# Scale rows loaded earlier, another matmul order in a wave's last step, and four normalizations moved to VectorE

## The chip, the cores and the metric

The kernel runs on one core of a Trainium2 chip. The metric is the device time of one execution in microseconds (us); the time before is 2232.88 us, the median of 3 runs (2232.68 to 2235.79). The profile is of one execution, with a span of 2227.6 us.

## What is computed

Input `u` has 2048 rows (tokens) of 1024. Three residual layers follow each other, each on the normalized rows:

```
x = u
x = x + 0.5 * ffn(layernorm(x))
x = x + s4(layernorm(x))
x = x + 0.5 * ffn(layernorm(x))          # the same weights as in the first

ffn(x) = (silu(x @ Wg) * (x @ Wu)) @ Wd  # Wg, Wu: 1024 x 2752, Wd: 2752 x 1024
W[k, n] = scale[k // 128, n] * (w4[k, n] - (z4[k // 128, n] + 1))
```

The weights of the feed-forward layers are packed 4-bit integers; each group of 128 rows of a weight has a scale and a zero point of its own for each column. `s4` is a causal convolution along the 1024 columns with a kernel that is computed from a state-space model's parameters, plus a multiple of its input.

## The kernel before

**Jobs.** The rows are cut into four blocks of 512. A job is one feed-forward layer of one block; `JOBS` (L1159) lists eight: first layers of blocks 0 and 1, then their last layers, then the same for blocks 2 and 3. `fast` (L1161) walks through them. Each has an up part (`gate_up`, L526) and a down part (`down`, L603). Smaller work is hung onto their steps as hooks: `at(up, s, f)` runs `f` as step `s` of the up part is written, `at(dn, s, f)` the same in the down part. The convolution of a block's middle layer, the residual adds and the normalization for the next job are such hooks.

**Group scales as ratios.** The products of a group of 128 rows must be scaled by that group's scale. The kernel multiplies the running sum in PSUM by the ratio of this group's scale to the next one's, after each group. So after each step each sum is read from its PSUM bank, multiplied and written back (`scaled`, L520), on ScalarE or on VectorE in turn. The ratios are in the table `rat`, made by `scales` (L288): TensorE transposes rows of scales that `scale_rows` (L281) loaded, VectorE copies them (L306), guards and inverts them (L277 to L279) and multiplies neighbours (L311, L312).

**Waves and steps.** The 2752 columns of gate and up are 21 blocks of 128 and a half one. A wave is three blocks of gate and the same three of up (waves 0 to 4), or two and two (waves 5 to 7; wave 7 has the half block as a fifth unit). Each such 128-column unit has one of six PSUM banks. A wave has eight steps, one for each group of 128 rows. In a step each unit gets two products: the input is split into a high part (fp32r, tile `xTh`) and a low rest (fp16, `xTl`), and each is multiplied with the weights. The order of these is the list `turns` (L543 to L545): for the first half of the units low, then high; for the second half high, then low. So a six-unit step is written as three low, six high and three low products. A unit is scaled when its second product is done.

**The end of a wave.** In a wave's last step (`g == GK - 1`) the units aren't scaled but go in pairs to `gated` (L576): ScalarE makes silu of the gate (L578), VectorE multiplies it with the up unit into `hf` (L581), GpSimd makes a rounded copy `hh` (L583) and the rest `hl` (L585). `hf` has two buffers, `g` three. The next wave's units take the banks in the same order.

**The down part** has 44 steps: for each half of the output columns one step for each of 22 blocks, with four sums of 128 columns, each of two products (`hl`, `hh`) and a scaling.

**Job 0** also makes the weights. Packed rows are loaded and split into nibbles on VectorE, reduced by the zero points (`dequantize`, L432; `dequantize_down`, L465) and written to DRAM (`wq`, `wdq`), from where every job's steps load them, four steps ahead. `first_weights` (L475) sets the steps at which this happens. The ratios are hooks of job 0 as well: for blocks 0 to 2 in `start` (L1270), for blocks 3 to 8, 9 to 14 and 15 to the end at steps 4, 20 and 36 (L1210), with the rows loaded in the same hook. They are first needed at steps 8 (wave 1), 24 (wave 3) and 40 (wave 5).

**Normalizing the next block.** `normalized` (L188) subtracts the mean and multiplies by the inverse deviation, a 128 x 1024 tile at a time, on an engine that can be given. For the next job's first layer `anorm` (L1233) calls it at the down steps; in job 0 (`pool`) it runs on GpSimd, and so does the split into high and low parts in `turn` (L204, `by_pool`); in the other jobs on VectorE. TensorE then transposes the tile (L198).

**Order.** The program is written in one order, and a framework places the instructions of each engine: it takes those that it reckons ready, the earlier written first, so that the placed order can differ from the written one. It also sets all waits. Where the order has to be kept, `in_order_of_writing` (L120) adds dependences along an engine; `start` runs under it for ScalarE, VectorE and SyncE.

Of the kernel before, what the change touches and what calls it, by code (L numbers as in the profile page):

```python
# [16 lines left out]
ALU = mybir.AluOpType  # L17
# [13 lines left out]
GK = 8  # L31
GD = 21
TW = 6
WIDE = INTER // P
# [18 lines left out]
def macaron_s4_kernel(  # L53
# [31 lines left out]
    nc = tc.nc  # L85
# [34 lines left out]
    def in_order_of_writing(f, *engines):  # L120

        start = len(nc.cur_bb.bb.instructions)
        f()
        written = list(nc.cur_bb.bb.instructions)
        for e in engines:
            last = next((i for i in reversed(written[:start]) if i.engine == e), None)
            for ins in written[start:]:
                if ins.engine == e:
                    if last is not None:
                        tc.add_manual_dep(  # L130
                            ins,
                            last.name,
                            mybir.DependencyInfo(
                                mybir.DependencyClass.NoSync, mybir.DependencyReason.DATA
                            ),
                            reason="order of writing",
                        )
                    last = ins


    x = {}
# [43 lines left out]
        for t in range(NT):  # L185
            ln[b, t] = (mv[:, t, 0:1], r[:, t : t + 1], k)

    def normalized(b, t, engine=nc.vector):  # L188
        m, r, k = ln[b, t]
        n = t4(f"xn_{b}_{k}_{t}")  # L190
        engine.tensor_scalar(n, x[b][t], m, r, ALU.subtract, ALU.mult)  # L191
        return n

    def turned(n, name, bank=bank):
# [331 lines left out]
    def gate_up(j, b, hooks):  # L526
        hi, lo = pieces[b]
        ps = {}
        ready = {s: load_w(j, s) for s in range(AHEAD)}
        for s, (wi, g) in enumerate(STEPS):  # L530
            if s + AHEAD < len(STEPS):
                ready[s + AHEAD] = load_w(j, s + AHEAD)
            for hook in hooks.get(s, ()):
                hook()
            w = ready.pop(s)
            fs = WAVES[wi]
            n = len(fs)
            order = [(2 * f + i, i * n + u) for u, f in enumerate(fs) for i in range(2)]
            if wi == len(WAVES) - 1:
                order.append((2 * WIDE, 2 * n))  # L540


            early = len(order) // 2  # L543
            turns = [(k, pos, k == 1) for k in range(2) for pos in range(early)]
            turns += [(k, pos, k == 0) for k in (1, 0) for pos in range(early, len(order))]  # L545
            for k, pos, done in turns:
                unit, col = order[pos]
                if g == 0 and unit not in ps:
                    ps[unit] = acc(f"pg_{j}_{unit}")
                p = ps[unit]  # L550
                weights = w[:, bass.ts(col, P)]
                if k == 0:

                    weights = weights.bitcast(BF16).rearrange("p (n k) -> p k n", k=2)[:, 1, :]
                nc.tensor.matmul(  # L555
                    p,
                    weights,
                    (lo, hi)[k][:, g, :],
                    start=(g == 0 and not done),
                    stop=(g == GK - 1 and done),  # L560
                    skip_group_check=True,
                )
                if not done:
                    continue
                if g < GK - 1:
                    on_act = unit % 2 == 0 or (j == 0 and pos == 1)
                    if unit == 2 * WIDE:
                        on_act = g % 2 == 0
                    scaled(on_act, p, p, rat[:, unit, g : g + 1])
                elif unit == 2 * WIDE:  # L570
                    gated_half(j, ps.pop(unit))
                elif unit % 2:
                    gated(j, unit // 2, ps.pop(unit - 1), ps.pop(unit))
        pieces.pop(b)
# [586 lines left out]
    def fast():  # L1161
        for j, (b, k) in enumerate(JOBS):
            prev = JOBS[j - 1] if j else None
            after = JOBS[j + 1] if j + 1 < len(JOBS) else None
            up, dn = {}, {}

            def at(hooks, s, f):
                hooks.setdefault(s, []).append(f)

            if prev:  # L1170
                pb, pk = prev
                for t in range(NT):
                    at(up, t, lambda t=t: back(pb, 1, t))
                if pk == 1:
                    late = 30 if j == 1 else 0
                    at(up, 4, lambda: moments(pb, 2))
                    at(up, 5, lambda: deviations(pb, 2))
                    s4x, s4n = {}, {}

                    def norm(t):  # L1180
                        s4n[t] = normalized(pb, t)

                    def swap(t):
                        s4x[t] = turn_whole(s4n.pop(t), f"st_{pb}_{t}")

                    def conv(t):
                        convolve(pb, t, s4x.pop(t), f"{pb}_{t}")

                    for t in range(NT):
                        at(up, late + 8 + 4 * t, lambda t=t: norm(t))  # L1190
                        at(up, late + 10 + 4 * t, lambda t=t: swap(t))
                        at(up, late + 12 + 4 * t, lambda t=t: conv(t))
                    at(up, late + 27, lambda: moments(pb, 3))
                    at(up, late + 28, lambda: deviations(pb, 3, LIFT))

                    def save():
                        for t, dst in enumerate(saved(pb)):
                            nc.sync.dma_start(dst, x[pb][t])

                    at(up, late + 28, save)  # L1200
                else:

                    def store():
                        for t, dst in enumerate(rows_of(out, pb)):
                            nc.sync.dma_start(dst, x[pb][t])
                        x.pop(pb)

                    at(up, 4, store)
            if j == 0:
                for s, k0, k1 in ((4, 3, 9), (20, 9, 15), (36, 15, WIDE)):  # L1210
                    at(up, s, lambda k0=k0, k1=k1: scales(k0, k1, scale_rows(k0, k1)))
                at(up, 40, scales_down)
                for t in range(NT):
                    at(up, t, lambda t=t: in_order_of_writing(lambda: second_half(t), *STARTING))
                first_weights(up, dn, at)
            if j == 1:
                tables = s4_tables()
                for s in range(2, 42):
                    at(up, s, lambda: next(tables, None))
            if j == 2:  # L1220
                at(up, 30, in_order)
            if after:
                ab, ak = after
                if ak == 1:
                    at(up, 55 if j == 0 else 6, lambda: load_x(ab, rows_of(u, ab)))
                    stage, o = (dn, 0) if j == 0 else (up, 44)
                    at(stage, o, lambda: in_order_of_writing(lambda: moments(ab, 1), ET.DVE))
                    at(stage, o + 1, lambda: deviations(ab, 1, LIFT))
                an = {}

                pool = j == 0

                def anorm(t):  # L1233
                    an[t] = normalized(ab, t, nc.gpsimd if pool else nc.vector)

                o = 3 if j == 0 else 0
                for t in range(NT):
                    at(dn, o + 1 + 4 * t, lambda t=t: anorm(t))
                    at(dn, o + 2 + 4 * t, lambda t=t: turn(ab, t, an[t][:, :512], 0, by_pool=pool))
                    at(dn, o + 4 + 4 * t, lambda t=t: turn(ab, t, an[t][:, 512:], 1, by_pool=pool))  # L1240
            at(dn, 21, lambda: load_x(b, rows_of(u, b) if k == 1 else saved(b)))
            for t in range(NT):
                at(dn, NF + 5 + 4 * t, lambda t=t: back(b, 0, t))
            gate_up(j, b, up)
            down(j, b, dn)
        b = JOBS[-1][0]
        for t, dst in enumerate(rows_of(out, b)):
            back(b, 1, t)
            nc.sync.dma_start(dst, x[b][t])

    STARTING = ET.Activation, ET.DVE, ET.SP
# [18 lines left out]
    def start():  # L1270
# [5 lines left out]
        srow = scale_rows(0, 3)  # L1276
        zeros_down = zero_words(1)
        fetch(1)
        zero_points(0, zeros)
        fetch_zeros(0)  # L1280
        fetch_zeros(1)
# [17 lines left out]
            less_mean(t, 1)  # L1299
        scales(0, 3, srow)  # L1300
        zero_points(1, zeros_down)

    in_order_of_writing(start, *STARTING)
    x.pop(0)
    fast()
    x.clear()
# [85 lines left out]
```

## Time and profile before

| | |
|---|---|
| time | 2232.88 us |
| TensorE busy | 2121.1 us of 2227.6 |
| VectorE busy | 1705.0 us |
| ScalarE busy | 1431.1 us |
| GpSimd busy | 383.4 us |
| scaling of gate and up sums, ScalarE (L522) | 1264 at 661 ns |
| the same on VectorE (L524) | 1144 at 695 ns |
| hf on VectorE (L581) | 168 at 749 ns |
| hh and hl on GpSimd (L583, L585) | 168 each, at 640 and 1345 ns |

In the profile's lines PE is TensorE, DVE VectorE, ACT ScalarE, POOL GpSimd; PEld is TensorE loading weights, SPq the queue of SyncE, which issues most DMAs. A line of the timeline has the start in us, the busy time in us, engine, line of the code, operation, what is written and what is read, the number of instructions merged into it, and in brackets the idle time before it and what ended that. A line of the waits has who waited and for whom, the sum in us, how often, and the longest. An answer on one tile has for each form the shortest, median and longest duration in ns. Matmuls are pipelined and overlap in the records, so that a step is measured from start to start.

### The profile page before, as it was taken

The numbers are of one execution on the slowest core, as the hardware profiler recorded it, in microseconds if no ns is written. First come the engines' busy times: TensorE is split into PE (matmuls) and PEld (weight loads), VectorE is DVE, ScalarE is ACT, GpSimd is POOL, SyncE is SP. The second block draws the span as 40 slices with busy tenths as digits, with TensorE's granted clock in tenths as the row PEclk, the third lists the DMA queues.
The fourth block names the chain that finished last, engine by engine and source line by source line (L and its number), as shares of the span: only waits on it lengthen the run. The fifth ranks groups of instructions, "written<-read, shape, count | busy, mean of one in ns | idle before, by whom it ended". The sixth has DMA issues, their size and how long they took to land.

```text
span 2227.6 us, 28004 instructions
## 1 busy us (share of the span) xinstructions
PE 2121.1 (95%) x9524; PEld 1424.2 (64%) x9524; DVE 1705.0 (77%) x2799; ACT 1431.1 (64%) x2245; POOL 383.4 (17%) x393
## 2 busy tenths in 40 slices
PE   5888889999999999999999999999999999999998
PEld 3444565566777657755685557776587765865576
DVE  7887768867886878777877788867788677777776
ACT  6667667545764577666766667646776467766675
POOL 0222511221001220022102220012300122012210
PEclk9999989999999999999999999999999999999999
DMA  7777675424443544543645454434444354454443
GB/s 251 255 248 264 200 237 167 154 93 145 145 154 115 174 137 151 190 141 115 211 152 180 128 167 133 154 117 158 137 133 156 117 172 137 156 190 142 131 133 121
DMA packets 163669, 359.93 MB, mean 162 GB/s; under 512 B 22395, under 2 KB 27572, under 8 KB 163518
## 3 DMA queue, kind: packets, MB, share of 16 engines
q1 hardware_dynamic: 162670, 356.50, 49.6%
q8 instruction: 78, 1.28, 0.2%
q10 hardware_dynamic: 592, 1.16, 0.1%
q0 software_dynamic: 256, 0.39, 0.1%
q14 instruction: 73, 0.60, 0.1%
HBM read 306.86 MB, written 50.73 MB: 161 GB/s over the span
## 4 chain that ended last, share of the span: by engine, by line
PE 78%; issue 7%; DVE 7%; POOL 5%; DMA 2%; ACT 2%; SPq 0%; ACTq 0%; DVEq 0%; POOLq 0%
PE pg L555 44%; PE po L617 26%; PE pc L914 3%; POOL hl L585 3%; PE pc L895 1%; DVE hf L581 1%; POOL hh L583 1%; PE pb L638 1%; PE pt L198 1%; ACT pg L522 1%; DVE q L437 1%; DVE pg L524 1%; POOL xn L191 1%; DVE po L524 1%; PE st L198 1%
## 5 line engine op out<-in xcount | busy, mean ns | idle before, releaser
L522 ACT ACTIVATE pg<-pg,rat 128x512 f32<-128x512 f32 x1264 | 801.4, 661 | 493.8 <-PE pg L555 474.3
L524 DVE TENSOR_TENSOR pg<-pg,rat 128x512 f32<-128x512 f32 x1144 | 765.2, 695 | 186.9 <-PE pg L555 181.0
L555 PE MATMUL pg<-xTh,w 128*128 128x512 f32 x2752 | 876.2, 443 | 19.7 <-DVE hf L581 13.9
L555 PE MATMUL pg<-xTl,w 128*128 128x512 f16 x2752 | 731.4, 383 | 33.9 <-ACT pg L522 14.1
L555 PEld LDWEIGHTS pg<-xTh,w 128*128 128x128 f32 x2752 | 520.0, 190 | 221.8 <-DVE hf L581 27.6
L617 PE MATMUL po<-hl,wd 128*128 128x512 f32 x1344 | 542.9, 405 | 9.0 <-DMA wd<-wdq 4.2
L522 ACT ACTIVATE po<-po,ratd 128x512 f32<-128x512 f32 x670 | 438.7, 663 | 162.8 <-PE po L617 162.2
L617 PE MATMUL po<-hh,wd 128*128 128x512 f32 x1344 | 528.2, 395 | 0.0
L524 DVE TENSOR_TENSOR po<-po,ratd 128x512 f32<-128x512 f32 x610 | 421.1, 698 | 110.0 <-PE po L617 106.2
L555 PEld LDWEIGHTS <-w 128*128 128x128 bf16 x2752 | 226.4, 99 | 352.0 <-issue 170.4
L583 POOL CAST hh<-hf 128x512 fp32r<-128x512 f32 x168 | 107.6, 640 | 1535.1 <-DVE hf L581 957.1
L617 PEld LDWEIGHTS po<-hl,wd 128*128 128x128 f32 x1344 | 255.3, 190 | 83.9 <-DVE po L524 15.9
L617 PEld LDWEIGHTS po<-hh,wd 128*128 128x128 f32 x1344 | 255.5, 190 | 47.5
L585 POOL TENSOR_TENSOR hl<-hf,hh 128x512 fp32r<-128x512 f32 x168 | 225.9, 1345 | 13.5
L581 DVE SCALAR_TENSOR_TENSOR hf<-pg,rat,g 128x512 f32<-128x512 f32 x168 | 124.0, 749 | 87.8 <-ACT g L578 44.0
L578 ACT ACTIVATE g<-pg,rat 128x512 f32<-128x512 f32 x168 | 111.3, 688 | 49.7 <-PE pg L555 48.9
L198 PE MATMUL pt<-ident,xn 128*128 128x128 f32 x256 | 45.3, 293 | 22.2 <-POOL xn L191 11.1
L161 DVE BATCH_NORM_STATS2 stats<-x 128x6 f32<-128x512 f32 x96 | 63.7, 679 | 1.1
L198 PEld LDWEIGHTS pt<-ident,xn 128*128 128x128 f32 x256 | 34.3, 150 | 33.7 <-ACT xn L1262 13.3
L221 DVE TENSOR_TENSOR xTl<-pt,xTh 128x512 f16<-128x512 f32 x56 | 38.4, 690 | 13.6 <-ACT xTh L220 13.1
L640 DVE TENSOR_TENSOR x<-x,pb 128x512 f32<-128x512 f32 x64 | 43.3, 680 | 5.4 <-PE pb L638 5.0
L220 ACT CAST xTh<-pt 128x512 fp32r<-128x512 f32 x56 | 33.0, 590 | 18.9 <-PE pt L198 18.8
(152 smaller groups left out, 831.1 us busy)
## 6 DMA issues: line engine op xcount, KB each, us to landing
w<-wq SPq DMA_DIRECT2D x319, 384.0 KB
wd<-wdq SPq DMA_DIRECT2D x336, 256.0 KB
w<-wq SPq DMA_DIRECT2D x128, 256.0 KB
w<-wq SPq DMA_DIRECT2D x64, 320.0 KB
x<-in_L_attn_u_dram SPq DMA_DIRECT2D x30, 512.0 KB
wq<-q SPq DMA_DIRECT2D x40, 384.0 KB
wdq<-qd SPq DMA_DIRECT2D x32, 256.0 KB
xs<-x SPq DMA_DIRECT2D x16, 512.0 KB
```

The costliest lines, as they stand in the source:

```text
L161: nc.vector.bn_stats(stats[:, t, i, :], x[b][t][:, bass.ts(i, 512)])
L198: nc.tensor.transpose(ps[:, bass.ts(k, P)], n[:, bass.ts(k, P)], ident)
L522: nc.scalar.activation(dst, src, AF.Copy, scale=sc)
L524: nc.vector.tensor_tensor(dst, src, sc.to_broadcast([P, TB]), ALU.mult)
L555: nc.tensor.matmul(p, weights, (lo, hi)[k][:, g, :], start=(g == 0 and not done), stop=(g == GK - 1 and done), skip_group_check=True,)
L578: nc.scalar.activation(g, pg, AF.Silu, scale=rat[:, 2 * f, GK - 1 :])
L581: nc.vector.scalar_tensor_tensor(hf, pu, last, g, ALU.mult, ALU.mult)
L583: nc.gpsimd.tensor_copy(hi, hf)
L585: nc.gpsimd.tensor_tensor(lo, hf, hi.bitcast(F32), ALU.subtract)
L617: nc.tensor.matmul(ps[c], w[:, bass.ts(c, P)], part, start=(f == 0 and k == 0), stop=(f == NF - 1), skip_group_check=True,)
L640: nc.vector.tensor_tensor(part, part, ps, ALU.add)
L914: nc.tensor.matmul(dst, lhsT, rhs, start=start, stop=stop, skip_group_check=True)
```

## The change

Three things. The rows of scales are loaded ahead: those for blocks 3 to 8 in `start`, the others five steps before `s`, and the ratios are made two steps before `s`, where `s` is now 4, 16 and 32: loads at the start, at 11 and at 27, ratios at steps 2, 14 and 30. It is to have the ratios ready when their waves begin. In the last step of a wave all low products are written first, then all high ones, so that all units end in the second half of the step. And `normalized` is always on VectorE; job 0's splitting in `turn` stays on GpSimd.

```diff
@@ in_order_of_writing
         start = len(nc.cur_bb.bb.instructions)
-        f()
+        got = f()
         written = list(nc.cur_bb.bb.instructions)
...
+        return got
@@ normalized
-    def normalized(b, t, engine=nc.vector):
+    def normalized(b, t):
         m, r, k = ln[b, t]
         n = t4(f"xn_{b}_{k}_{t}")
-        engine.tensor_scalar(n, x[b][t], m, r, ALU.subtract, ALU.mult)
+        nc.vector.tensor_scalar(n, x[b][t], m, r, ALU.subtract, ALU.mult)
@@ gate_up
             turns += [(k, pos, k == 0) for k in (1, 0) for pos in range(early, len(order))]
+            if g == GK - 1:
+                turns = [(k, pos, k == 1) for k in range(2) for pos in range(len(order))]
             for k, pos, done in turns:
@@ fast
             if j == 0:
-                for s, k0, k1 in ((4, 3, 9), (20, 9, 15), (36, 15, WIDE)):
-                    at(up, s, lambda k0=k0, k1=k1: scales(k0, k1, scale_rows(k0, k1)))
+                rows = {3: srow_next}
+                for s, k0, k1 in ((4, 3, 9), (16, 9, 15), (32, 15, WIDE)):
+                    if k0 > 3:
+                        load = lambda k0=k0, k1=k1: rows.update({k0: scale_rows(k0, k1)})
+                        at(up, s - 5, load)
+                    at(up, s - 2, lambda k0=k0, k1=k1: scales(k0, k1, rows.pop(k0)))
@@ fast, anorm
-                    an[t] = normalized(ab, t, nc.gpsimd if pool else nc.vector)
+                    an[t] = normalized(ab, t)
@@ start
         fetch(1)
+        rows_next = scale_rows(3, 9)
         zero_points(0, zeros)
...
         zero_points(1, zeros_down)
-
-    in_order_of_writing(start, *STARTING)
+        return rows_next
+
+    srow_next = in_order_of_writing(start, *STARTING)
```

## The prediction

> **What bounds the kernel now.** The page first: which engine carries the chain of work that ended last.
>
> ```profile
> PE 2121.1 (95%) x9524; PEld 1424.2 (64%) x9524; DVE 1705.0 (77%) x2799; ACT 1431.1 (64%) x2245; POOL 383.4 (17%) x393
> PE 78%; issue 7%; DVE 7%; POOL 5%; DMA 2%; ACT 2%; SPq 0%; ACTq 0%; DVEq 0%; POOLq 0%
> ```
>
> TensorE is the bound. From the matmul starts in the timeline a step of six units (12 matmuls) takes 2.70 us and a step of four units (8) takes 1.80 us where nothing is awaited, so the change is worth what it takes from or adds to TensorE's waits. The same starts give the jobs: job 0 runs from 29.2 to 346.1 us (its up part 200.2, its down part 116.7), while jobs 3, 4 and 7 need about 165 and 85. Job 0 is where 66 us lie open, and two of the three edits touch job 0 alone.
>
> The waits of 56.5 to 64 us (start of wave 1 of job 0), then VectorE's timeline there:
>
> ```profile
> ACT pg L522 <- DVE rat L311: 6.3, 1, 6.3
> PE pg L555 <- ACT pg L522: 4.8, 1, 4.8
> ...
> 57.93 1.33 DVE L277 TENSOR_TENSOR sq<-s_gu 128x96 f32<-128x96 f32 x1
> 60.54 1.31 DVE L278 SCALAR_TENSOR_TENSOR inv<-sq,s_gu 128x96 f32<-128x96 f32 x1
> 61.89 0.75 DVE L279 RECIPROCAL inv<-inv 128x96 f32<-128x96 f32 x1
> 62.68 0.25 DVE L311 TENSOR_TENSOR rat<-s_gu,inv 128x84 f32<-128x84 f32 x1
> ```
>
> The ratios of wave 1 are ready at 62.9, after wave 1 has begun; ScalarE's first scaling waits for them, and TensorE for ScalarE. Also to be seen: the code writes this at step 4, yet it runs after step 7. The framework places the instructions of an engine itself, so a written order is not yet a placed one.
>
> The waits of 229.4 to 346 us (down part of job 0), and the two forms of line 191 in the answer on tile xn:
>
> ```profile
> PEld pt L198 <- POOL xn L191: 12.3, 3, 4.7
> PE pt L198 <- POOL xn L191: 11.1, 3, 4.4
> ...
> L191 DVE TENSOR_SCALAR xn<-x,mv,r x40: 803/806/1183, 454.7 to 1810.0; 128x1024 f32<-128x1024 f32 x40
> L191 POOL TENSOR_SCALAR xn<-x,mv,r x4: 3778/4260/4987, 250.2 to 279.2; 128x1024 f32<-128x1024 f32 x4
> ```
>
> TensorE stood 11.1 us for four normalizations at 4.26 us; the same one takes VectorE 0.81.
>
> Last, the timeline at the end of a wave in a quiet job (job 3, wave 0 to 1):
>
> ```profile
> 940.67 1.43 DVE L581 SCALAR_TENSOR_TENSOR hf<-pg,rat,g 128x512 f32<-128x512 f32 x2 [0.79 <-ACT g L578]
> 941.48 0.61 POOL L583 CAST hh<-hf 128x512 fp32r<-128x512 f32 x1 [104.41 <-PE pg L555]
> 942.17 1.29 POOL L585 TENSOR_TENSOR hl<-hf,hh 128x512 fp32r<-128x512 f32 x1
> 943.50 0.75 DVE L581 SCALAR_TENSOR_TENSOR hf<-pg,rat,g 128x512 f32<-128x512 f32 x1 [1.40 <-POOL hl L585]
> 944.17 0.69 DVE L524 TENSOR_TENSOR pg<-pg,rat 128x512 f32<-128x512 f32 x1
> 944.31 0.50 PE L555 MATMUL pg<-xTh,w 128*128 128x512 f32 x1 [0.82 <-DVE hf L581]
> ```
>
> A wave has three pairs but hf has two buffers. The third hf waits until GpSimd is done with the first; the third pair's bank stays taken; TensorE stands 0.82 us, and the step takes 3.80 instead of 2.70.
>
> [...] after the waits at 63.7, 169.2, 264.0 and 284.0 it shows half clock, and the mean from 262 to 290 is 0.76. [...] the scaling at 944.17 was held behind the waiting hf. [...] 1024 elements in 0.81 us, where a 512-element product takes 0.70. [...] dequantizations qd of 0.68 us took 1.32 and 1.83 while GpSimd was busy (250.6, 257.7), and the sq and inv above took 1.3 where the first set of ratios (26.0, GpSimd without elementwise work) took 0.20 each.
>
> **The scale rows (job 0).** Two DMA issues move to the start: SyncE idles there from 8.8 to 11.9 us, which hides their 0.3 us each; the others replace equal issues in place. Removed: the late ratios. Wave 1's first two steps took 7.86 and 4.17 us, those of wave 2, which had no late ratios, 3.78 and 2.84: 5.4 us. Wave 3 against wave 4, three steps: 12.05 against 9.90, 2.2 us. Wave 5 against wave 6, three steps: 12.9 against 7.1, 5.8 us. Sum 13.4, half clock included. Given back: the chain still costs VectorE, in the middle of a wave where GpSimd is quiet, about 0.25+0.25+0.25+0.75+0.25+0.25 = 2 us, three times. VectorE is busy 21.0 of 27.3 us in wave 0 and 22.3 of 26.5 in wave 3, so I let 0.5 us each reach TensorE: 1.5. And at the head of wave 6 TensorE waits 3.2 us for weights whose dequantization keeps to the same steps; if wave 5 gets faster, part of the wait grows: I take 4 back, between 0 and 6. Net 8 us, from 5 to 13.
>
> **The normalizations (job 0).** Removed: 2.44+4.37+4.32 = 11.1 us, and the half clock after them: of 255.1-258.6, 264.0-268.8 and 284.0-289.3, half of 3.5+4.8+5.3, so 6.8. Together 17.9. Steps 8 to 24 take 51.4 us now. Added: 4 x 0.81 = 3.2 us on VectorE, between dequantizations. Queued behind them are the scalings, for which TensorE waits. VectorE's work per step here: 1.2 dequantizations x 0.84 + 1.25 scalings x 0.70 + 0.2 = 2.1 us, against 2.05 for TensorE with the transposes (2.17 and 1.93 in turn in job 1). VectorE becomes the bound, at 2.2 us a step: 17 x 2.2 = 37.4. Gain 14, from 8 (2.55 us a step) to 18. GpSimd keeps eight pairs of cast and difference, 16.3 us; they don't bind.
>
> **The order in a wave's last step (all jobs).** In the six-unit waves the first unit ends three low products later: 3 x 0.216 = 0.65 us. Its hf, GpSimd's cast and difference, and the third hf move with it: 943.50 becomes 944.15 to 944.2. In addition the first up unit's bank is freed by its hf at 942.1 instead of 941.4, where the next wave wants it at 941.75. If the placed order stays as it is, each such wave end costs 0.7 us. But TensorE need not stand: in jobs 2, 5 and 6 a normalization sits in front of the first hf at the end of wave 0 (1442.3), and there the framework placed the third pair's high product behind five more low products and the waiting hf behind a scaling; the wait for hf is then 0.02 us with 0.3 elsewhere, where job 3 has 1.1. The delay that made it do so was at most that normalization's 0.8; the new order makes one of 0.65 at every wave end, so I expect such a placement at most of them. It gains some 0.5 against the shift of 0.7: net 0.2. Over 26 open six-unit ends (5 each in jobs 3, 4, 7; 3 each in jobs 2, 5, 6, where convolutions of 6.7 us cover the other two; 2 in jobs 0 and 1 together) that is 5 us; nothing for the four-unit ends and the way into the down part if they are placed anew too, 0 to 13 if not. I take +8, with 0 and +31 as ends.
>
> Sum: 2233 - 8 - 14 + 8 = 2219 us.
>
> **Rivals.**
> *The written order is also the placed one: slower.* 26 x 0.7 = 18; four-unit ends 16 x 0.45 (first low product of the second pair waits 0.27 for its scaling, then the second hf comes 0.45 later) = 7; into the down part 8 x 0.8, since the half tile's hf at 2136.0 waits for GpSimd's 2135.98 = 6. That is +31, more than job 0 gives back if the two edits there bring their small ends or a little more, 13 to 20: 2244-2251; I take 2245. For: the steady steps of jobs 3 to 7 are placed as written. Against: the placement in jobs 2, 5, 6.
> *VectorE and the weights take back most of job 0.* Normalizations 5, scales 5, order +6: 2229, about no change. For: VectorE busy 22.2 of 25.7 us from 229.4 on. Against: steps 12 to 15 already run at 2.1 us beside the same dequantizations.
> *All of it.* Scales 12, normalizations 17, order +1: 2205. For: the waits are plain in the trace. Against: DMA share 0.84 to 0.87 in waves 6 and 7.
>
> **How the numbers follow.** Chances: main case 0.50, slower 0.22, taken back 0.14, all 0.14. Faster: nearly all of the main case (0.47), all of the last, 0.07 of the taken-back one: 0.68; slower 0.22; the rest 0.10. The range, 2201 to 2246, reaches to both outer cases.
>
> **What would show it.** Right: no wait of ScalarE for the ratios of line 311 after 50 us; no GpSimd row of line 191; job 0 shorter by about 20 us, no half clock from 255 to 290; first steps of waves in jobs 3, 4 and 7 between 3.8 and 4.1 us, with high products placed late. Wrong: those steps at 4.5 with the order unchanged (the slower rival), or steps 8 to 24 of job 0's down part at 2.5 us with TensorE waiting for line 524 (taken back).

## The result and the profile after

The changed kernel takes 2212.7 us (median of 4 runs, 2211.28 to 2214.65), against 2233.11 for the kernel before in the same comparison: a ratio of 0.9907, 95% interval 0.989 to 0.9924, or 20.8 us less (17 to 25). The forecast was 2219.0, range 2201 to 2246. The sum came out near; two of its three terms did not, as the parts below show. The two traced executions took 2229.41 and 2211.56 us, so the parts read from the traces add up to some 18 us and not to 20.8.

The page of the changed kernel, line 1 and line 4:

```profile
PE 2121.7 (96%) x9524; PEld 1416.0 (64%) x9524; DVE 1703.2 (77%) x2803; ACT 1425.0 (64%) x2245; POOL 367.8 (17%) x389
PE 54%; issue 24%; DVE 4%; POOL 4%; DMA 1%; ACT 1%; SPq 0%; POOLq 0%; DVEq 0%; ACTq 0%
```

TensorE is still the bound, with the same busy time to 0.6 us. What became shorter is its idle time. The second line is a warning: "issue" rose from 7 to 24% and PE fell from 78 to 54%, while the kernel became faster. So these shares are not read as waiting here; the waits and the starts of the matmuls are.

**Job by job**, in us from matmul start to matmul start (up part / down part; job 7's down part up to the end of its last matmul):

| | before | after |
|---|---|---|
| job 0 | 200.2 / 116.7 | 200.2 / 104.4 |
| jobs 1, 2 | 209.3 / 85.3, 192.0 / 85.2 | 209.9 / 85.4, 192.0 / 85.6 |
| jobs 3, 4 | 165.6 / 85.5, 165.5 / 85.4 | 163.0 / 85.4, 163.0 / 85.5 |
| jobs 5, 6 | 190.2 / 85.2, 190.1 / 85.3 | 189.9 / 85.7, 189.9 / 85.6 |
| job 7 | 162.8 / 85.1 | 161.5 / 85.2 |

Job 0's down part gives 12.3 us, the other jobs some 5 (6.2 in their up parts, less 1.2 in their down parts), and job 0's up part, the place of the scale rows, nothing.

**Job 0's up part.** The waits of the kernel before from 29.2 to 229.4 us, then those of the changed kernel from 28.7 to 228.9 us:

```profile
ACT pg L522 <- DVE rat L311: 16.7, 3, 6.3
PE pg L555 <- ACT pg L522: 13.3, 4, 4.8
...
PE pg L555 <- DMA w<-wq: 7.9, 7, 3.2
...
PE pg L555 <- DVE hf L581: 1.5, 3, 1.1
```

```profile
PE pg L558 <- DMA w<-wq: 10.4, 8, 2.7
PE pg L558 <- DVE hf L584: 9.0, 5, 4.0
...
PE pg L558 <- DVE pg L525: 5.1, 6, 1.6
```

In the changed kernel no row has ScalarE waiting for `rat` any more; before it was 16.7 us, and TensorE waited 13.3 for ScalarE, 13.0 of it in three waits behind `rat`. But TensorE now waits 9.0 for `hf` (before 1.5), 10.4 for weights (before 7.9) and 5.1 for VectorE's scalings (before 3.1). In between, from 82.3 to 89.7 us, VectorE's timeline shows where the ratios went, and TensorE's what that did:

```profile
82.37 0.26 DVE L307 COPY s_gu<-ps_s 128x96 f32<-128x96 f32 x1 [1.40 <-PE ps_s L296]
82.55 0.74 DVE L584 SCALAR_TENSOR_TENSOR hf<-pg,rat,g 128x512 f32<-128x512 f32 x1
83.21 0.95 DVE L438 TENSOR_TENSOR q<-even,z 128x768 fp32r<-128x768 uint8 x1
84.07 0.67 DVE L278 TENSOR_TENSOR sq<-s_gu 128x96 f32<-128x96 f32 x1
84.66 0.95 DVE L438 TENSOR_TENSOR q<-raw,z 128x768 fp32r<-128x768 uint8 x1
85.53 1.31 DVE L279 SCALAR_TENSOR_TENSOR inv<-sq,s_gu 128x96 f32<-128x96 f32 x1
86.76 0.17 DVE L313 TENSOR_SCALAR rat<-s_gu 128x12 f32<-128x12 f32 x1
86.84 0.74 DVE L584 SCALAR_TENSOR_TENSOR hf<-pg,rat,g 128x512 f32<-128x512 f32 x1
87.50 0.73 DVE L280 RECIPROCAL inv<-inv 128x96 f32<-128x96 f32 x1
88.16 0.65 DVE L584 SCALAR_TENSOR_TENSOR hf<-pg,rat,g 128x512 f32<-128x512 f32 x1
88.73 0.97 DVE L312 TENSOR_TENSOR rat<-s_gu,inv 128x84 f32<-128x84 f32 x1
```

```profile
87.63 0.50 PE L558 MATMUL pg<-xTh,w 128*128 128x512 f32 x1 [2.58 <-DVE hf L584]
88.86 0.50 PE L558 MATMUL pg<-xTh,w 128*128 128x512 f32 x1 [0.72 <-DVE hf L584]
```

Written at step 14, the ratios of wave 3 are made at the end of wave 1, between the three `hf` products with which wave 1 hands over its banks. The first step of wave 2 takes 6.56 us, before 3.78. Those of wave 5 (written at step 30) sit the same way at the end of wave 3 (`inv` at 142.18, `hf` at 144.25): the first step of wave 4 takes 7.86, before 4.04. Wave by wave, in these two traces, waves 1, 3 and 5, which had waited for ratios, became 2.3, 1.4 and 5.1 us shorter, and waves 2 and 4 became 4.8 and 2.2 us longer, with 1.8 more in waves 0, 6 and 7: the sum is nothing.

**Job 0's down part.** The waits of the changed kernel from 228.9 to 333.3 us, and one form in the answer on tile `xn`:

```profile
PE po L620 <- DVE po L525: 4.6, 7, 1.6
```

```profile
L192 DVE TENSOR_SCALAR xn<-x,mv,r x44: 791/805/1400, 250.8 to 1793.5; 128x1024 f32<-128x1024 f32 x44
```

The 11.1 us of waiting for GpSimd are gone with its four rows; the 44 normalizations are all on VectorE. TensorE's waits for VectorE's scalings rose from 1.1 to 4.6 us. The windows view over this part, of the kernel before and of the changed one (span, then busy time of PE, PEld, DVE, ACT, POOL, the granted TensorE clock, DMA share, GB/s):

```profile
229.40:346.10 116.70, 98.90 (x393) 74.09 (x393) 78.72 (x135) 74.82 (x122) 36.63 (x23) 0.90 0.67 215
```

```profile
228.90:333.30 104.40, 94.27 (x393) 69.19 (x393) 81.27 (x137) 74.23 (x122) 22.44 (x19) 0.95 0.75 239
```

GpSimd lost 14.2 us, VectorE gained 2.6, and the clock rose from 0.90 to 0.95: the waits of 4.37 and 4.32 us, after which it was 0.52 from 264 to 269 and 0.50 from 284 to 289.3 us, are gone, and from 250 to 290 us the changed kernel shows 1.00.

**The end of a wave in job 3**, VectorE, GpSimd and TensorE of the changed kernel, to be read beside the prediction's last view:

```profile
929.62 1.41 DVE L584 SCALAR_TENSOR_TENSOR hf<-pg,rat,g 128x512 f32<-128x512 f32 x2 [1.47 <-ACT g L581]
...
931.13 1.27 POOL L588 TENSOR_TENSOR hl<-hf,hh 128x512 fp32r<-128x512 f32 x1
931.27 0.70 DVE L525 TENSOR_TENSOR pg<-pg,rat 128x512 f32<-128x512 f32 x1 [0.24 <-PE pg L558]
931.76 0.76 PEld L558 LDWEIGHTS <-w 128*128 128x128 bf16 x5 [0.27 <-issue]
931.76 1.25 PE L558 MATMUL pg<-xTl,w 128*128 128x512 f16 x5
...
932.43 0.75 DVE L584 SCALAR_TENSOR_TENSOR hf<-pg,rat,g 128x512 f32<-128x512 f32 x1 [0.47 <-POOL hl L588]
...
933.24 0.50 PE L558 MATMUL pg<-xTh,w 128*128 128x512 f32 x1 [0.22 <-DVE hf L584]
```

The third `hf` still waits for GpSimd. But a scaling (931.27) now goes ahead of it, five low products (931.76) lie in front of the high product that needs its bank, and TensorE stands 0.22 us instead of 0.82. The first two steps of the wave take 2.84 + 3.23 us, before 3.80 + 2.70.

### The profile page after: what moved, and what is told of

Same layout as the page of the kernel before. It is cut to its first block, busy times and chain, and to the rows that moved or that the text cites. A ratio compares the mean times of both kernels' runs of the same rounds, so it can differ in the third digit from the quotient of the medians.

```text
span 2209.8 us, 27967 instructions
## 1 busy us (share of the span) xinstructions
PE 2121.7 (96%) x9524; PEld 1416.0 (64%) x9524; DVE 1703.2 (77%) x2803; ACT 1425.0 (64%) x2245; POOL 367.8 (17%) x389
## 4 chain that ended last, share of the span: by engine, by line
PE 54%; issue 24%; DVE 4%; POOL 4%; DMA 1%; ACT 1%; SPq 0%; POOLq 0%; DVEq 0%; ACTq 0%
PE pg L558 32%; PE po L620 15%; PE pc L917 3%; POOL hl L588 3%; PE pc L898 1%; DVE hf L584 1%; POOL hh L586 1%; PE pb L641 1%; PE st L199 1%; DVE pg L525 1%; DMA wd<-wdq 1%; ACT g L581 0%; PE pt L199 0%; DVE po L525 0%; DVE qd L470 0%
## 5 line engine op out<-in xcount | busy, mean ns | idle before, releaser
L558 PE MATMUL pg<-xTl,w 128*128 128x512 f16 x2752 | 744.4, 384 | 19.0 <-DMA w<-wq 10.4
L588 POOL TENSOR_TENSOR hl<-hf,hh 128x512 fp32r<-128x512 f32 x168 | 222.6, 1325 | 13.4
L199 PE MATMUL pt<-ident,xn 128*128 128x128 f32 x256 | 43.0, 285 | 11.1 <-ACT xn L1269 11.1
L222 DVE TENSOR_TENSOR xTl<-pt,xTh 128x512 f16<-128x512 f32 x56 | 38.3, 689 | 14.6 <-ACT xTh L221 14.4
L641 PE MATMUL pb<-ident,y 128*128 128x128 f32 x256 | 42.5, 279 | 3.5 <-DVE x L643 3.4
```

The costliest lines, as they stand in the source:

```text
L199: nc.tensor.transpose(ps[:, bass.ts(k, P)], n[:, bass.ts(k, P)], ident)
L558: nc.tensor.matmul(p, weights, (lo, hi)[k][:, g, :], start=(g == 0 and not done), stop=(g == GK - 1 and done), skip_group_check=True,)
L588: nc.gpsimd.tensor_tensor(lo, hf, hi.bitcast(F32), ALU.subtract)
L641: nc.tensor.transpose(ps[:, bass.ts(c, P)], yT[a, c][:, bass.ts(t, P)], ident)
```

## The experiments

All ratios are to the kernel before, measured beside it on the same chip; a difference in us is (ratio - 1) x 2233. The intervals in brackets reach some 1.5 to 4 us either way, and two kernels of different comparisons are told apart only where their intervals are apart.

### The parts one by one

Three kernels have one part of the change each, and one has all but the scale rows.

*The scale rows alone:*

```diff
-                for s, k0, k1 in ((4, 3, 9), (20, 9, 15), (36, 15, WIDE)):
-                    at(up, s, lambda k0=k0, k1=k1: scales(k0, k1, scale_rows(k0, k1)))
+                rows = {3: srow_next}
+                for s, k0, k1 in ((4, 3, 9), (16, 9, 15), (32, 15, WIDE)):
...
+                        at(up, s - 5, load)
+                    at(up, s - 2, lambda k0=k0, k1=k1: scales(k0, k1, rows.pop(k0)))
```

> The kernel before with only the scale rows and ratios moved. My theory (the waits for ratios were traded for a ratio chain that the framework places at the ends of waves 1 and 3, in front of the hf products): within 3 us of before, the up part of job 0 at 198 to 202 us, waves 2 and 4 of job 0 longer than before and waves 1 and 5 shorter. Rival (the edit alone gains its 8 us or more, and the new order in a wave's last step took that back in job 0): 2220 to 2226 us, the up part at 188 to 192.

Measured: 2235.57 us, ratio 1.0018 (1.0012 to 1.0025), so 4 us slower, where at most 3 was expected. Job 0's up part took 206.3 us, more than the 198 to 202 expected; waves 2 and 4 became longer and waves 1 and 5 shorter, as expected. TensorE's waits for ScalarE are gone there, but it waits 9.1 us for `hf` and 14.7 for weights. So the loss isn't a matter of the other two edits: the wait that is removed comes back elsewhere in job 0's up part.

*The order alone:*

```diff
+            if g == GK - 1:
+                turns = [(k, pos, k == 1) for k in range(2) for pos in range(len(order))]
```

> The kernel before with only the new order in a wave's last step. My theory (the framework places the third pair's high product later, which gains a little more than the later hf costs): 2226 to 2231 us; wave 1 of jobs 3, 4 and 7 at 22.3 us against 22.7, their down parts 0.1 to 0.4 longer. Rival (the order costs time at the wave ends, and the measured gain is all from the other two edits): 2235 us or more.

Measured: 2225.47 us, ratio 0.9972 (0.9961 to 0.9982), 6.3 us faster (4 to 9). Jobs 3, 4 and 7 have up parts of 163.0, 162.9 and 161.4, as in the whole change. The order's gain needs neither of the other parts.

*The normalizations alone:*

```diff
-                    an[t] = normalized(ab, t, nc.gpsimd if pool else nc.vector)
+                    an[t] = normalized(ab, t)
```

> The kernel before with only the four normalizations of job 0 on VectorE. My theory: 2219 to 2223 us, the down part of job 0 at 104 to 106 us instead of 116.7, everything else as before. Rival (the shorter down part came from an up part that delivers its weights differently): 2227 to 2231 us.

Measured: 2221.1 us, ratio 0.9947 (0.9934 to 0.996), 11.8 us faster (9 to 15); job 0's down part 103.2, a little below the range.

This trace also warns. Job 0's up part has the same code as in the kernel before, and yet it took 203.2 us instead of 200.2. Other pairs of kernels here with the same code for that part took 199.7 and 201.9 (the order alone, the change without the scale rows), 200.2 and 200.0 (the change, and the change with its order forced), and 196.7 and 203.1 (a third `hf` buffer, without and with the moved normalizations). So a difference of a few us between two such up parts, each traced once, shows nothing. TensorE's waits for `hf` there agree within 0.5 us in all four pairs, and can be compared.

*The change without the scale rows* (the first diff of this section undone in it):

```diff
-                for s, k0, k1 in ((4, 3, 9), (16, 9, 15), (32, 15, WIDE)):
...
-                    at(up, s - 2, lambda k0=k0, k1=k1: scales(k0, k1, rows.pop(k0)))
+                for s, k0, k1 in ((4, 3, 9), (20, 9, 15), (36, 15, WIDE)):
+                    at(up, s, lambda k0=k0, k1=k1: scales(k0, k1, scale_rows(k0, k1)))
```

> The changed kernel (2212.7 us) with the scale rows as before: order and normalizations only. Alone, the order was worth 6.5 us and the normalizations 10.9 us, the rows cost 3.6; the whole change is worth 20.4, so that 3.0 us is left for the rows in the company of the others. Theory (the three parts don't add up; in this company the rows bring some 3 us): 2214 to 2218 us, with TensorE waiting 8 to 13 us for ScalarE in job 0's up part. Rival 1 (the rows cost what they cost alone; the others bring more together): 2207 to 2211. Rival 2 (the forecast 8 us): 2219 to 2223.

Measured: 2212.16 us, ratio 0.9911 (0.9898 to 0.9925), 19.9 us faster. That falls between the first two expectations and well away from the third: within some 4 us, which is what these intervals allow, the whole gain is that of the order and the normalizations (6.3 + 11.8 = 18.1 apart), and no gain of the scale rows can be seen. Its waits in job 0's up part show that they could have brought something:

```profile
ACT pg L522 <- DVE rat L311: 15.7, 3, 6.5
PE pg L557 <- DMA w<-wq: 9.0, 6, 3.9
PE pg L557 <- ACT pg L522: 8.9, 3, 5.1
...
PE pg L557 <- DVE hf L583: 2.7, 3, 1.7
```

### Why the scale rows bring nothing

*The ratios four steps earlier,* so that each chain is written away from the end of a wave: at steps 10 and 26, with the loads at 7 and 23.

```diff
-                for s, k0, k1 in ((4, 3, 9), (16, 9, 15), (32, 15, WIDE)):
+                for s, k0, k1 in ((4, 3, 9), (12, 9, 15), (28, 15, WIDE)):
```

> The changed kernel with loads and ratios of blocks 9 to 14 and 15 to the end four steps earlier still (loads at steps 7 and 23, ratios at 10 and 26), so that the ratio chain falls into the middle of waves. My theory (what took the gain back is the chain standing in front of hf at the wave end): 2204 to 2208 us, waves 2 and 4 of job 0 at 25 to 27 us instead of 30.7 and 27.5. Rival (the weights, made and loaded at the same steps, take it back wherever the chain stands): 2210 to 2214 us, with the wait moved to the loads of w.

Measured: 2208.95 us, ratio 0.9898 (0.9884 to 0.9913), by the ratios 2 us below the whole change, which is not clear of noise. It lies between the two expected ranges. The chain of wave 3 now runs in the middle of wave 1, at the price that the prediction had set; VectorE's timeline of this kernel:

```profile
71.24 0.25 DVE L278 TENSOR_TENSOR sq<-s_gu 128x96 f32<-128x96 f32 x1
71.52 0.26 DVE L279 SCALAR_TENSOR_TENSOR inv<-sq,s_gu 128x96 f32<-128x96 f32 x1
71.81 0.75 DVE L280 RECIPROCAL inv<-inv 128x96 f32<-128x96 f32 x1
```

That of wave 5 still ran late (`sq` at 134.3), though it was written at step 26: its half block's row, which `scales` itself loads, was transposed only at 133.5. The waits for `hf` fell from 9.0 to 4.7, those for weights rose from 10.4 to 12.9, and the up part took 198.5 us instead of 200.2. Waves 2 and 4 took 28.4 and 23.3 us, where 25 to 27 was expected. So the place of the chain matters for the wait for `hf`, by about half of it. That the time gains by it is not shown by this kernel, since both its 2 us and the 1.7 us of the up part are within the scatter; the kernels with a third buffer, below, decide this.

*The two chains left out:* in the changed kernel the ratios of blocks 9 to 21 are not made.

```diff
-                    at(up, s - 2, lambda k0=k0, k1=k1: scales(k0, k1, rows.pop(k0)))
+                    if k0 == 3:
+                        at(up, s - 2, lambda: scales(3, 9, rows.pop(3)))
+                        at(up, s - 2, lambda: nc.vector.memset(rat[:, 18:], 1.0))
+                        at(up, s - 2, lambda: nc.vector.memset(s_gu[:, 18:], 1.0))
```

> The changed kernel (2212.7 us) without the making of the ratios of blocks 9 to 21: the loads of their rows stay, the transposes, copies, inversions and products are left out, and the table gets ones in their place (so these columns are scaled wrongly). It shows how much of job 0's up part the chain at the ends of waves 1 and 3 costs. Theory (the chain in VectorE's queue between the hf products is what replaced the removed wait): TensorE's waits for hf in job 0's up part fall from 9.0 to at most 3 us, its wave 2 and wave 4 begin with steps below 4 us, the up part falls from 200.2 to 190-194 us and the time to 2203-2208. Rival (the weights' transfers set job 0's pace and take back what the chain leaves): hf waits fall, waits for weights rise by as much, the up part stays at 197-201 and the time at 2209-2214.

Measured: 2207.4 us, ratio 0.9895 (0.9879 to 0.9912), 2.7 us below the whole change by the ratios, again not clear of noise. The time is in the first range and the up part, 198.0 us, in the rival's; since that is the part at issue, and the ratio too gives less than the 5 us expected, the first theory falls as the whole explanation. The first step of wave 4 came down to 4.28 us (7.86), that of wave 2 only to 5.90 (6.56). Its timeline at the end of wave 1 shows why; VectorE, then TensorE:

```profile
81.69 0.75 DVE L584 SCALAR_TENSOR_TENSOR hf<-pg,rat,g 128x512 f32<-128x512 f32 x1 [1.47 <-ACT g L581]
82.36 0.95 DVE L438 TENSOR_TENSOR q<-even,z 128x768 fp32r<-128x768 uint8 x1
83.22 0.75 DVE L584 SCALAR_TENSOR_TENSOR hf<-pg,rat,g 128x512 f32<-128x512 f32 x1
83.88 0.95 DVE L438 TENSOR_TENSOR q<-raw,z 128x768 fp32r<-128x768 uint8 x1
85.99 0.75 DVE L584 SCALAR_TENSOR_TENSOR hf<-pg,rat,g 128x512 f32<-128x512 f32 x1 [1.15 <-POOL hl L588]
...
86.79 0.51 PE L558 MATMUL pg<-xTh,w 128*128 128x512 f32 x1 [2.27 <-DVE hf L584]
```

With no ratio in the way, two dequantizations stand between the `hf` products, and the third waits 1.15 us for GpSimd to give back one of the two `hf` buffers. So the chain is one of several works in that queue. TensorE's waits for it in job 0's up part, from the waits view of each kernel (us):

| kernel | ScalarE's scaling | `hf` | weights | VectorE's scaling | up part |
|---|---|---|---|---|---|
| before | 13.3 | 1.5 | 7.9 | 3.1 | 200.2 |
| change without rows | 8.9 | 2.7 | 9.0 | 1.5 | 201.9 |
| whole change | 1.0 | 9.0 | 10.4 | 5.1 | 200.2 |
| ratios earlier | 0.1 | 4.7 | 12.9 | 3.0 | 198.5 |
| two chains left out | 0.2 | 4.8 | 12.1 | 4.8 | 198.0 |

(The 1.0, 0.1 and 0.2 are sums of the single waits in the trace, most of them too short for that view.)

### What the order does

*The written order forced.* In the changed kernel, in jobs 2 to 7, dependences keep TensorE's products as written through a wave's last step and the next two.

```diff
+                for ins in list(nc.cur_bb.bb.instructions)[begun:]:
+                    if ins.engine == ET.PE:
+                        if kept:
+                            tc.add_manual_dep(ins, kept[-1].name, ...)
+                        kept.append(ins)
```

> The changed kernel, but in jobs 2 to 7 TensorE's products of the last step of a wave and the first two of the next keep their written order. My theory (the third pair's high product must step back for the later hf to cost nothing): the first step of a wave in jobs 3, 4 and 7 takes 4.4 to 4.6 us (3.8 before, plus 0.7), 2228 to 2237 us in all. Rival (GpSimd's pace sets the wave end whatever TensorE's order is): the first two steps still sum to about 6.1 us, 2210 to 2216 us.

Measured: 2242.6 us, ratio 1.0053 (1.0033 to 1.0074). The first step of waves 1 to 4 in job 3 is 4.45 us and the second 2.71. The total was above the range, since wave 5 of jobs 3 and 4, a four-unit wave with other work hung in, took 20.3 us instead of 15.8. TensorE's timeline at the end of job 3's wave 0:

```profile
930.77 1.50 PE L560 MATMUL pg<-xTh,w 128*128 128x512 f32 x5
933.57 0.51 PE L560 MATMUL pg<-xTh,w 128*128 128x512 f32 x1 [1.30 <-DVE hf L601]
```

The two steps over such an end are thus 7.16 us as written (4.45 + 2.71), 6.50 in the kernel before (3.80 + 2.70), and 6.07 as placed (2.84 + 3.23): the edit itself costs 0.66, and the new placement gives back 1.09.

*A third buffer for `hf`,* in the kernel before and in the changed one (with one buffer of `h` less, to make room):

```diff
-tc.tile_pool(name="hf", bufs=2)
+tc.tile_pool(name="hf", bufs=3)
-tc.tile_pool(name="h", bufs=2 * NF)
+tc.tile_pool(name="h", bufs=2 * NF - 1)
```

> The kernel before with three hf buffers instead of two, and 43 h buffers instead of 44 to make room. My theory (the wave end waits because the third hf needs a buffer that GpSimd still reads): first steps of waves in jobs 3, 4 and 7 at 2.7 to 2.9 us instead of 3.8, the kernel at 2205 to 2213 us. Rival (VectorE's or ScalarE's own work at the wave end is the next limit, hardly later): first steps at 3.4 us or more, 2225 to 2233 us.

> The changed kernel with three hf buffers and 43 h buffers. My theory: with the wait for GpSimd gone the new order has nothing left to gain and its later first pair costs a little: 0.1 to 0.4 us more per wave end than in the kernel before with three buffers; 2196 to 2206 us, since job 0's down part keeps its 12 us. Rival (the new order has a merit of its own): the first two steps of a wave shorter than with the old order and three buffers.

Measured: 2200.02 us, ratio 0.9857 (0.984 to 0.9874), and 2198.63 us, ratio 0.9845 (0.9828 to 0.9863). The first by itself brings 32 us, more than the whole change and more than expected. Job 3's end of wave 0 in it:

```profile
933.57 2.30 DVE L581 SCALAR_TENSOR_TENSOR hf<-pg,rat,g 128x512 f32<-128x512 f32 x3 [0.78 <-ACT g L578]
...
933.76 1.47 PE L555 MATMUL pg<-xTl,w 128*128 128x512 f16 x6
934.88 1.74 PE L555 MATMUL pg<-xTh,w 128*128 128x512 f32 x6
936.45 1.47 PE L555 MATMUL pg<-xTl,w 128*128 128x512 f16 x6
```

Three `hf` products in a row, TensorE without a gap, steps of 2.70 us throughout. With the changed kernel's order on top, the first step is 2.87 us in job 3; in jobs 2, 5, 6 and 7 the four-unit wave 5 takes 15.1 instead of 14.6. The up parts of jobs 1 to 7 add up to 1258.5 us with the new order and to 1249.7 with the old one: with a third buffer the order costs 9 us.

### Put together

Three kernels combine the third buffer with the other parts: all of the change, with the earlier ratios; the same with the old order; and normalizations only. From the first to the second:

```diff
-            if g == GK - 1:
-                turns = [(k, pos, k == 1) for k in range(2) for pos in range(len(order))]
```

From the second to the third, in which the rows are also loaded in the same hook again:

```diff
-                for s, k0, k1 in ((4, 3, 9), (12, 9, 15), (28, 15, WIDE)):
+                for s, k0, k1 in ((4, 3, 9), (20, 9, 15), (36, 15, WIDE)):
```

> The changed kernel with the ratios four steps earlier and three hf buffers. If the two effects lie in different places they add: 5 us below the changed kernel with three buffers, 2190 to 2201 us. If job 0's weights are the limit of its up part once the wave ends are shorter: no faster than that kernel.

> All edits of the version with early ratios and three hf buffers (2190.4 us) but the order in a wave's last step, which stays the old one. Theory (the order pays only by making the framework place the wave's end anew where a hf buffer is short; with three buffers it costs its shift): the up parts of jobs 1 to 7 lose the 9 us by which the two versions with three buffers differed, first steps of waves in jobs 3, 4 and 7 at 2.70 instead of 2.87: 2179 to 2185 us. Rival (the gain of 5 to 8 us that the order brought on its own is independent of the buffers): 2195 to 2199.

> The kernel before with three hf buffers and the normalizations on VectorE; scale rows and order as before. Theory (normalizations are worth 11 to 13 us whatever the up part does, early ratios some 7 more once hf has a free buffer): 2187 to 2191 us, job 0's up part 195 to 199, its down part 102 to 105, and the kernel without the new order but with early ratios 5 to 8 us below this one. Rival (without the hf waits the ratios' chain no longer matters and the weights' transfers set job 0's pace): this one equal to that within 3 us.

Measured:

| kernel, all with three `hf` buffers | us | ratio (95%) | job 0 up |
|---|---|---|---|
| earlier ratios, normalizations, new order | 2190.38 | 0.981 (0.9793 to 0.9828) | 192.2 |
| earlier ratios, normalizations, old order | 2180.95 | 0.9769 (0.9754 to 0.9784) | 193.3 |
| normalizations, old order | 2188.96 | 0.9799 (0.9786 to 0.9813) | 203.1 |

The order costs 9 us here (first row against the second), and the ratios made early are worth 7 to 8 (second against third; the intervals are just apart). The job 0 column says more than it should: the third kernel's trace is of the slowest of its five runs, 5.9 us above its median, and its up part of 203.1 was expected at 195 to 199. The first row, against the changed kernel with a third buffer, is the cleanest test of the chain's place, since only the steps of the loads and the ratios differ and both ran in one comparison: with the ratios at steps 14 and 30 the time is 2198.63 us (2196.33 to 2199.03), at steps 10 and 26 it is 2190.38 (2188.34 to 2191.09), 8 us less. The kernel with the ratios at 14 and 30 has a chain that runs from the end of wave 1 into wave 2, and though `hf` has its buffer a scaling stands behind that chain; VectorE, then TensorE:

```profile
92.17 1.29 DVE L312 TENSOR_TENSOR rat<-s_gu,inv 128x84 f32<-128x84 f32 x1
93.39 1.28 DVE L525 TENSOR_TENSOR pg<-pg,rat 128x512 f32<-128x512 f32 x2
...
94.13 1.09 PE L558 MATMUL pg<-xTh,w 128*128 128x512 f32 x3 [2.25 <-DVE pg L525]
```

TensorE's waits for `hf` in job 0's up part sort the two causes: 9.0 us in the change, 4.7 with the ratios earlier, 3.4 with a third buffer, 0.5 with both. So the scale rows gain about their forecast 8 us, but only with ratios made in the middle of a wave and, as far as these runs can tell, a third `hf` buffer.

The second is the fastest kernel of this study, 52 us below the kernel before. Its waits in job 0's up part (29.3 to 222.6 us) name what is left there:

```profile
PE pg L556 <- DMA w<-wq: 17.3, 11, 4.0
...
PE pg L556 <- DVE pg L525: 1.8, 2, 1.2
```

Neither ratios nor `hf`, but the weights. TensorE's wait for them grows as others go: 7.9 us before, 12.1 to 17.3 in the kernels without late ratios that wait for `hf` less than the changed one does.

## Why the prediction was right in sum and wrong in parts

| term | forecast | measured |
|---|---|---|
| scale rows | -8 (-13 to -5) | about 0 in the change: -20.8 with them, -19.9 without; +4.0 alone |
| normalizations | -14 (-18 to -8) | -12.3 in job 0's down part; -11.8 (-15 to -9) alone |
| order | +8 (0 to +31) | -6.3 (-9 to -4) alone |
| sum | -14 | -20.8 (-25 to -17) |

**Scale rows: a step failed.** What is removed was nearly right: the starts of waves 1, 3 and 5 that the forecast counted became 11.6 us shorter, where it had 13.4. The step that failed is "the chain still costs VectorE, in the middle of a wave where GpSimd is quiet, about ... 2 us", of which 0.5 each was to reach TensorE. The chains came at the ends of waves 1 and 3, while GpSimd made `hh` and `hl`, and took 4.1 us of VectorE's time at the first of them (0.26 + 0.67 + 1.31 + 0.17 + 0.73 + 0.97), amid the `hf` products. Steps 14 and 30, where they are written, are already the seventh of eight in their waves; only step 2 is in the middle of one. And they were placed later still: TensorE transposed the first of them at 81.8 us, in the wave's last step. The prediction had itself read that "a written order is not yet a placed one", and among the chains used it for the old one only. Putting the chain earlier, or leaving two of the three out, took the waits for `hf` from 9.0 to 4.7 and 4.8, so that about half of them is the chain's. A third `hf` buffer took them to 3.4, and both to 0.5; that dequantizations in the same queue have a part is read from the timeline and was not tried apart. The other step, "I take 4 back" for the weights, was right in kind: they rose by 2.5 in the whole change and by 6.8 with the rows alone. What sets the time of these transfers was not tried and stays open.

**Normalizations: right in kind, with the pace and one count off.** 11.1 us of waiting went, and with it about half of the time at half clock (the mean clock rose from 0.90 over 116.7 us to 0.95 over 104.4). The forecast sets 51.4 us against 17 x 2.2 = 37.4 for steps 8 to 24. By the matmul starts these 17 steps took 53.2 us before; 51.3 is 16 of them, 8 to 23. Its own argument thus gave a gain of 15.8 and not 14. After the change the 17 steps take 39.9 us, 2.35 each instead of 2.2, so that they gain 13.3, and the steps outside them lose 1.0. One step of 4.36 us and two of 2.74 and 3.23 lie well above the 2.2; in the first TensorE waits 1.6 us for VectorE's scalings. VectorE does become what TensorE waits for (4.6 us in the part, before 1.1), as forecast, and takes a few us of the gain, not the 9 of the rival. That 12.3 is so near to 14 is in part the luck of the miscount.

**Order: right mechanism, mis-sized term.** The shift was put at 0.7 us and is 0.66 (the forced order against the kernel before). That the placement would be made anew, with the high product late, came true at these wave ends. The mis-sized term is "it gains some 0.5": it gains 1.09, so that a wave end is 0.43 better, not 0.2 worse. The forecast seems to have taken the 0.5 from what TensorE stands visibly for `hf`, 0.82 before, less the 0.3 that jobs 2, 5 and 6 showed. But the whole first step was 1.10 over 2.70, and after the change both steps together are only 0.67 over; that a scaling which no longer stands behind the waiting `hf` makes the rest is read from the timeline, not tried. Nor does the gain lie at 26 wave ends: with the order alone the up parts of jobs 3, 4 and 7 are 2.5, 2.6 and 1.4 us shorter, and those of jobs 2, 5 and 6 change by at most 0.2. The second thing left out was which conditions make the edit pay: it pays because `hf` has two buffers and costs 9 us when it has three.

**The rivals and the signs.** The order as written would have been slower than the kernel before, at 2242.6, near that rival's 2245, but in part by chance: in the forced kernel the up parts of jobs 2 to 7 are 26.2 us longer than before, and 8.5 of these lie in wave 5 of jobs 3 and 4, which the rival did not count. It fell because the placement was not as written, as the main case argued. "Taken back" came true for the scale rows only, in the whole change through the queue at the wave end (`hf` 7.5 us more) rather than the weights (2.5). "All of it" has no support: job 0 gave 12.3 us, not 29. Of the signs, no wait for ratios after 50 us, no GpSimd row of line 191, no half clock from 255 to 290, and high products late in the first step all held. Job 0 shorter by about 20 us did not (12.3), nor did first steps of 3.8 to 4.1 (2.84). The total was near by luck: the two errors, 8 us too much for the rows and 14 too little for the order, partly cancelled, which is no evidence for the size of either.

## What to carry to other kernels

When work is moved earlier, ask what it will stand between on its new engine queue, not only whether its result will be in time: here a chain made early at the end of a wave cost as much as one made late at its beginning. A reordering that only moves a wait about is a substitute for the buffer whose absence makes the wait; try the buffer first (32 us against 6 here), and try the reordering again once it is there, since its sign turned. And check a prediction's terms one by one: a sum that is right may hold two that are wrong.

## What the runs showed of the hardware

The small operations of the ratios took 0.25 us in one place and 1.31 in another. This is not a rate: VectorE's instruction ends right after GpSimd's. GpSimd and VectorE of the changed kernel from 142 to 144 us:

```profile
142.11 1.26 POOL L588 TENSOR_TENSOR hl<-hf,hh 128x512 fp32r<-128x512 f32 x1
```

```profile
142.18 1.31 DVE L279 SCALAR_TENSOR_TENSOR inv<-sq,s_gu 128x104 f32<-128x104 f32 x1
```

GpSimd ends at 143.37, `inv` at 143.49, 0.12 later. The other such operations that start while `hl` runs end likewise, among them 86.72 and 86.84, 89.60 and 89.70 in the changed kernel, 59.15 and 59.26, 61.74 and 61.85 in the kernel before. In the changed kernel a dequantization `qd` (0.68 us alone) that starts during a GpSimd operation ends 0.54 to 0.55 after it in 9 of 11 cases, at most 1.78 us long. In the other two (206.06 and 259.45) `qd` took 0.68, and GpSimd's operation, begun 0.03 and 0.31 us earlier, 1.86 and 2.14 instead of some 1.3. The scalings, which have one operand in PSUM, take 0.70 us either way (in the kernel before, 194 that start during GpSimd work, 950 others).

Beside GpSimd's normalizations most records show no such lengthening: in the kernel before `xn` runs on GpSimd from 258.99 to 263.98 and from 279.23 to 283.97 us, and four `qd` within these (259.47, 261.58, 279.72, 282.03) took 0.68 to 0.69 each, as alone. After the second and the fourth of them 1.7 and 1.3 us of the normalization were left, so that in these records both engines worked at the same time. A fifth, at 250.56 beside the normalization from 250.16 to 253.94, took 1.32. What makes the difference was not tried. The prediction put 0.25 us on most of the chain's small operations; beside `hl` one of them took up to 1.35 (`sq` at 163.42 in the kernel before).

No length of a single wait separates half clock from full clock in these traces. In the kernel before, after a wait of 2.44 us, matmuls came 0.43 us apart instead of 0.23 from 255.1 us on, and so they did from 237.1 after a wait of 1.64 in the changed kernel, while after a wait of 3.61 that ended at 116.95 in the kernel before they came 0.23 apart (clock 1.00 from 117 to 122). What besides the length of a wait decides was not tried.
